# A graph layer's edge loop: two edges of one target in one partition, and gathers without a wait for TensorE

## The chip, the cores and the metric

The kernel runs on one core of one Trainium2 chip. The metric is device microseconds of one execution. Engines are named as the profile names them: PE (TensorE's matmuls) and PEld (its weight loads), DVE (VectorE), ACT (ScalarE), POOL (GpSimd, which issues the indirect gathers) and SP (SyncE, which issues the other DMAs).

## The reference

12500 nodes have rows x of 128 floats. The 412500 edges are 200000 drawn pairs in both directions and one self loop for each node, sorted by their target dst. What is computed, cut to what matters:

```python
theta = x[dst] - x[src]
w = sigmoid(relu(theta @ W1 + b1) @ W2 + b2)
agg = segment_sum(w * theta, dst)
indeg = segment_sum(ones, dst)
out = layernorm(x + agg + indeg * (x @ W4 + b4))
```

A self loop has theta = 0, so it adds nothing to agg and one to indeg.

## The kernel before

**Tables.** theta @ W1 is the difference of two table rows. A first stage of 13 chunks makes two tables in DRAM: z, with x W1 beside x for each node (1 KB a row), which is gathered by source, and y3d, with x W1 cut into three bfloat16 parts, which is read by target.

**Steps and blocks.** The edges are cut into parts; one part is one step s of the main loop (NS = 352 steps). The first PLAIN = 20 parts hold 1024 edges each (FIRST and MORE), every later part CE = 1182. Two steps are a block b, whose targets fit a window of WB = 96 nodes. Steps s < NH = 8 gather from x itself, later ones from z.

**Placing.** For the later parts `place` (a generator whose pieces are strewn over the loop, three sets of up to 128 steps) thins each part of 1182 edges down to 1024 places, eight tiles (K = 8) of 128 partitions. It drops the self loops and takes out 128 "hot" edges, 64 from each of two ranges of 1152 sources, whose rows come from tables in SBUF by products with one-hot matrices (`hot_fetch`, L891) instead of a gather. What is left is squeezed together by eight passes of shifts (L565 to L581), and the sources (src_i), places in the window (rel) and places among the part's targets (rows_d in DRAM) are written out.

**A step.** For step s the engines do this:

- POOL: `gather` issues eight indirect DMAs (L340), 128 rows of z each, into one of NZ = 9 row buffers (zbuf), for step s + AHEAD = 4 in the order of the code.
- ACT: `one_hot` makes oh for step s + 2 in two passes (L772, L773) over the broadcast places (to_all, one DMA a block): 123 partitions by 9 x 128, eight tiles and one for the hot edges. There are two buffers oh.
- PE: `spread_y` multiplies oh with y3, a product for each of the eight tiles (L781): each edge's target row of x W1, in ph (PSUM, two buffers).
- DVE: `one_hot_w` makes ow (L791), 128 x 8 x 96, the edge's place in the block's window, in two buffers. `weights` subtracts the gathered rows from ph (L824), applies relu and W2 (L825) and sums (L828). ACT makes the gate from the sums by a sigmoid (L829, L830). `weigh` multiplies the gathered x with the gate into wx (L839, two buffers of 8 x 130 columns: 128 values, the gate and a constant 1).
- PE: `add_up` adds ow times wx into pa (L940), a product for each tile with 130 columns, and one for the hot edges (`hot_rows` L904 and L905, `hot_weights` L915 to L920). At a block's odd step a last product carries the former block's sums over (a times sh). `total` copies pa to a (ACT, L951), and `normalize` (L963 to L990) finishes the rows of the block two before and stores them.

**Order.** The code gives instructions a priority by their place; a scheduler fixes each engine's order at build time, except for SP's, which is written out by hand. Every engine then works its own queue in order, and a waiting instruction holds what stands behind it. Two rules are set by hand for gathers: they keep their own order, and from step NH + LAG on the gather of tile k of step s waits for a step of TensorE's work that was entered for (s - LAG, k), with LAG = 6. `step` enters these: the block's own transpose (L707), the last of spread_y's products, hot_rows' product (L905) and add_up's last. At the end a flag computed by the kernel from its own assumptions (`bad`) chooses whether a general path, `any_dst`, runs instead; line L1111.

Of the kernel before, what the change touches and what calls it, by code (L numbers as in the profile page):

```python
# [19 lines left out]
P = 128  # L20
D = 128
K = 8
BE = K * P
# [7 lines left out]
NZ = 9  # L31
AHEAD = 4
LB = 6
LAG = 6
# [8 lines left out]
RW = BE + HK  # L43
# [5 lines left out]
CE = 1182  # L49
# [7 lines left out]
def gnn_resnorm(  # L57
# [45 lines left out]
    KT = -(-TAIL // P)  # L103
    assert NS == NF + 1 and NS % SUB == 0 and TAIL <= BE and SUB == 2 and N < BIG

# [36 lines left out]
    def load(i):  # L142

        s0, n, full = sets[i]
        es = ep.tile([P, CE], I32, name="es")
        ed = ep.tile([P, CE + 1], I32, name="ed")
        e0 = E1 + (s0 - PLAIN) * CE
        if full < n:
            nc.vector.memset(es[:n, :], 0)
            nc.vector.memset(ed[:n, :], N)  # L150
# [68 lines left out]
    oh_buf = [const.tile([P, K + 1, P], BF16, name=f"oh{i}") for i in range(2)]  # L219
# [78 lines left out]
    wx_buf = [const.tile([P, K, AW], F32, name=f"wx{i}") for i in range(2)]  # L298
# [19 lines left out]
    def tiles(s):  # L318
        return K if s < NF else KT

# [8 lines left out]
    steps_of = {}  # L329
    table_steps = []  # L330

    def step(s, i, ins):

        steps_of[s // SUB * SUB + i // K, i % K] = ins

    def gather(s):

        (src_i, _, _), i = set_of(s)
        for k in range(tiles(s)):
# [7 lines left out]
            if s - LAG >= NH and (s - LAG, k) in steps_of:  # L347
                waits.append((steps_of[s - LAG, k], mybir.DependencyClass.Sync))
# [92 lines left out]
    def place(i, ps, es, ed, bb):  # L441
# [9 lines left out]
        c = ep.tile([P, 6], F32, name="col")[:n]  # L451
# [9 lines left out]
        v.tensor_scalar(b[:full, 1:2], c[:full, 3:4], -1.0, float(CE - BE - HR * HS),  # L461
                        op0=OP.mult, op1=OP.add)
# [5 lines left out]
        t = ep.tile([P, CE], F32, name="et")[:n]  # L468
        nc.scalar.activation(t, ed[:, :CE], AF.Identity, scale=float(BIG), bias=c[:, 0:1])
        C = CE // 3  # L470
        for j in range(3):
            at = slice(j * C, (j + 1) * C)
            step = ps.tile([P, G, P], F32, name=bank).rearrange("p g d -> p (g d)")[:n, :C]
            v.tensor_sub(step, ed[:, j * C + 1:(j + 1) * C + 1], ed[:, at])
            q = ep.tile([P, P * G], F32, name="eq")[:n, :C]
            v.tensor_sub(q, es[:, at], ed[:, at])
            v.tensor_mul(q, q, step)
            v.scalar_tensor_tensor(t[:, at], step, 0.0, t[:, at], op0=OP.is_equal, op1=OP.mult)
# [11 lines left out]
        key = ep.tile([P, CE + 1], F32, name="ed")[:n, :CE]  # L490
# [3 lines left out]
        for r in range(HR):  # L494
            apart = aparts[r][:n]
            whole = CE // PM * PM
# [3 lines left out]
                apart.rearrange("p (o m) -> p o m", o=1).to_broadcast([n, CE // PM, PM]), op=OP.add)  # L500
            if whole < CE:
                v.tensor_tensor(key[:, whole:], t[:, whole:], apart[:, :CE - whole], op=OP.add)
# [32 lines left out]
        nc.sync.dma_start(rows_d[:n, BE:], hd[:, 1, :])  # L535
        hots[s0] = hot_s, hrel, n

        w = ep.tile([P, CE], I32, name="ew")[:n]
        C = CE // 6
        for j in range(6):  # L540
            at = slice(j * C, (j + 1) * C)
            pw = ps.tile([P, G, P], F32, name=bank).rearrange("p g d -> p (g d)")[:n]
            count = pw[:, :C]
            q = ep.tile([P, P * G], F32, name="eq")[:n]
            keep, out_ = q[:, :C], q[:, C:2 * C]
            v.tensor_scalar(keep, t[:, at], float(NOT * BIG), None, op0=OP.is_ge)
            v.scalar_tensor_tensor(w[:, at], t[:, at], float((2 * NOT - 1) * BIG), keep,
                                   op0=OP.min, op1=OP.mult)
            v.tensor_scalar(out_, keep, -1.0, 1.0, op0=OP.mult, op1=OP.add)
            v.tensor_tensor_scan(count, out_, most[:n].to_broadcast([n, C]),  # L550
                                 c[:, 4:5] if j else 0.0, op0=OP.add, op1=OP.min)
            v.tensor_copy(c[:, 4:5], count[:, C - 1:])
            move = out_.bitcast(I32)
            far_on = pw[:, C:2 * C]
# [6 lines left out]
        v.tensor_sub(b[:full, 10:11], c[:full, 4:5], c[:full, 3:4])  # L561
        v.tensor_scalar(b[:full, 10:11], b[:full, 10:11], -float(HR * HS), None, op0=OP.add)
        v.tensor_scalar(b[:full, 11:12], b[:full, 10:11], -1.0, None, op0=OP.mult)
        assert SW + HR * HS < LAST + P
        for r, m in enumerate([1 << r for r in range(7)] + [LAST]):  # L565
            u = ep.tile([P, CE], I32, name="ew" if r % 2 else "et")[:n]
            C = bits.shape[1] - m
            for c0 in range(0, CE, C):
                c2 = min(c0 + C + m, CE)
# [9 lines left out]
                if c2 == CE:  # L579
                    break  # L580
            w = u  # L581
        to = ep.tile([P, CE + 1], I32, name="ed")[:n, :BE]
        v.tensor_scalar(to, w[:, :BE], BIG.bit_length() - 1, 2 * NOT - 1,
                        op0=OP.logical_shift_right, op1=OP.bitwise_and)
        off = ep.tile([P, P * G], F32, name="eq").bitcast(BF16)
        nc.scalar.activation(off[:n], to, AF.Identity, bias=c[:, 1:2])
        nc.sync.dma_start(rows_d[:n, :BE], off[:n])
        yield
        t = ep.tile([P, CE], F32, name="et")[:n]
        nc.scalar.activation(t[:, :BE], to, AF.Identity, bias=c[:, 2:3])  # L590
        src_i = pp.tile([P, K, P], I32, name="src_i")
        rel = pp.tile([P, K, P], BF16, name="rel")
        f = ep.tile([P, CE], F32, name="es")[:n]
# [3 lines left out]
        for e, to in ((f, src_i), (t, rel)):  # L597
            for k0 in range(0, K, G):
                pt = ps.tile([P, G, P], F32, name=bank)
                for j in range(G):  # L600
                    nc.tensor.transpose(pt[:, j, :n], e[:, (k0 + j) * P:(k0 + j + 1) * P],
                                        ident[:n, :n])
                nc.scalar.activation(to[:, k0:k0 + G, :n], pt[:, :, :n], AF.Copy)
                yield
        placed[s0] = src_i, rel, rows_d

    with tc.manual_schedule(engines={SP}), tc.tile_pool(name="work", bufs=2) as wp, tc.tile_pool(
# [94 lines left out]
        def own_u(b):  # L702
# [3 lines left out]
            step(b * SUB - 2, 2,  # L706
                 nc.tensor.transpose(pw[:, :WB], d["xw"][:WB], ident[:WB, :WB]))  # L707
# [42 lines left out]
        def one_hot(s, half):  # L750


            n0, n1 = half * G, min(half * G + G, tiles(s))
# [21 lines left out]
        def spread_y(s):  # L775

            d = parts[s]
            b, h = divmod(s, SUB)
            d["ph"] = ps_h.tile([P, K, D], F32, name="ph")
            for k in range(tiles(s) if s >= NH else 0):  # L780
                got = nc.tensor.matmul(d["ph"][:, k, :], d["oh"][:, k, :], blocks[b]["y3"][h],  # L781
                                       start=True, stop=True)
                if k == tiles(s) - 1:
                    step(s - 1, 9 * (1 - h), got)

        def one_hot_w(s):

            n = tiles(s)
            (_, rel, _), i = set_of(s)
            ow = wp.tile([P, K, WB], F32, name="ow", bufs=2)[:, :n, :]  # L790
            nc.vector.tensor_tensor(ow, iota_f.to_broadcast([P, n, WB]),  # L791
                                    rel[:, :n, i:i + 1].to_broadcast([P, n, WB]), op=OP.is_equal)
            parts[s]["ow"] = ow
# [17 lines left out]
        def weights(s):  # L811
            n = tiles(s)
            d = parts[s]
            zs = rows_of(s)
            xs = zs if s < NH else zs[:, :, D:]
            wx = wx_buf[s % 2]
            h = d["ph"]
            if s < NH:
                both(s)
                nc.vector.scalar_tensor_tensor(  # L820
                    h, d["ph"], 0.0, w2_f.to_broadcast([P, K, D]), op0=OP.max, op1=OP.mult)
            else:
                ph = d["ph"][:, :n, :]
                nc.vector.tensor_sub(ph, ph, zs[:, :n, :D])  # L824
                nc.vector.scalar_tensor_tensor(  # L825
                    h[:, :n, :], ph, 0.0, w2_f.to_broadcast([P, n, D]), op0=OP.max, op1=OP.mult)
            lg = wp.tile([P, K], F32, name="lg")
            summed = nc.vector.tensor_reduce(lg[:, :n], h[:, :n, :], AX.X, OP.add)  # L828
            nc.scalar.activation(gate[:, s % 2, :n], lg[:, :n], AF.Sigmoid, bias=b2_c)  # L829
            nc.scalar.activation(wx[:, :n, D], lg[:, :n], AF.Sigmoid, bias=b2_c)  # L830
            return summed

        def weigh(s):

            n = tiles(s)
            zs = rows_of(s)
            xs = zs if s < NH else zs[:, :, D:]
            w = gate[:, s % 2, :n].rearrange("p (k e) -> p k e", e=1)
            return nc.vector.tensor_tensor(wx_buf[s % 2][:, :n, :D], xs[:, :n, :],  # L839
                                           w.to_broadcast([P, n, D]), op=OP.mult)  # L840
# [57 lines left out]
        def hot_rows(s):  # L898
# [6 lines left out]
            got = nc.tensor.matmul(px[:, 0, :], d["oh"][:, K, :], blocks[b]["y3"][h],  # L905
                                   start=False, stop=True)
            step(s - 2, K * h + 7, got)
# [14 lines left out]
        def add_up(s):  # L922

            n = tiles(s)
# [6 lines left out]
            terms = [(d["ow"][:, k, :], wx_buf[s % 2][:, k, :]) for k in range(n)]  # L931
# [7 lines left out]
            for i, (one, w) in enumerate(terms):  # L939
                summed = nc.tensor.matmul(pa, one, w, start=h == 0 and i == 0,  # L940
                                          stop=h == 1 and i == len(terms) - 1)
            step(s + 1, (13, 5)[h], summed)
# [3 lines left out]
        def total(b):  # L946
# [4 lines left out]
            nc.scalar.activation(a[:WB], pa, AF.Copy)  # L951
# [4 lines left out]
            d.update(a=a, sw=sw[:WB, 0:1], deg=sw[:WB, 1:] if b * SUB >= PLAIN else a[:WB, D + 1:])  # L956
# [92 lines left out]
        for s in range(NS + 1):  # L1049
# [33 lines left out]
            if s + 2 < NS and tiles(s + 2) > G:  # L1083
# [14 lines left out]
        with after(weighted):  # L1098
# [201 lines left out]
```

## Time and profile before

| | us |
|---|---|
| three runs: lowest, median, highest | 4624.53, 4624.89, 4639.22 |
| profiled execution, whole | 4628.1 |
| its span, first to last instruction | 4626.2 |
| busy: DVE | 3121.2 (67%) |
| busy: POOL | 2681.1 (58%) |
| busy: PE, PEld | 2636.8 (57%), 1988.8 (43%) |
| busy: ACT | 1603.8 (35%) |
| mean granted TensorE clock | 0.729 |

PE and PEld overlap. A share is a mean over the whole span; the set-up before the regular loop lasts some 470 us. An idle time in the groups is the time that the engine stood still just before such an instruction, and the name behind it is who ended most of it; "remote" is an update of a semaphore that the profile cannot put to an instruction, "issue" a wait that it does not show.

### The profile page before, as it was taken

What the parts mean: (1) busy time and instruction counts of PE and PEld (TensorE: products, weight loads), DVE (VectorE), ACT (ScalarE), POOL (GpSimd) and SP (SyncE); (2) the same over time, 40 slices, a digit from 0 to 9 for tenths busy, and PEclk for the clock granted to TensorE, in tenths of its full rate; (3) what the DMA queues carried; (4) which work ended last, traced back from release to release, by engine and by line L of the source; (5) the groups of instructions that cost most, each with busy time, mean ns of one, the idle gap of its engine ahead of it and who ended that gap; (6) DMA issues with size and microseconds to landing.
All of it is one profiled execution on the core that took longest, in us unless ns stands there. A gap on an engine that the chain in (4) does not pass through costs nothing. (4 is left out here: it accounts for less than half of the span.)

```text
span 4626.2 us, 47225 instructions
## 1 busy us (share of the span) xinstructions
PE 2636.8 (57%) x14207; PEld 1988.8 (43%) x14207; DVE 3121.2 (67%) x5030; ACT 1603.8 (35%) x3344; POOL 2681.1 (58%) x2824
## 2 busy tenths in 40 slices
PE   4355556665655555655565655556555556555555
PEld 4344344444444444444444444444444444444444
DVE  5676667777776666666777776777666566566666
ACT  4233333333333333333333333333333333333333
POOL 4415656666565566665556656656656565655663
PEclk6676777767777777777777777776777777777777
DMA  6303433443443344434333433434433443333432
GB/s 247 111 28 108 126 115 114 122 121 112 118 122 110 109 125 122 120 114 122 112 118 116 121 109 115 123 111 123 121 112 112 121 120 117 116 116 114 120 113 67
DMA packets 269164, 539.42 MB, mean 117 GB/s; under 512 B 101349, under 2 KB 152737, under 8 KB 267365
## 3 DMA queue, kind: packets, MB, share of 16 engines
q0 software_dynamic: 134096, 364.95, 27.2%
q1 hardware_dynamic: 132834, 164.97, 11.2%
q10 hardware_dynamic: 1970, 6.40, 0.5%
q8 instruction: 115, 1.88, 0.2%
q14 instruction: 149, 1.21, 0.1%
HBM read 504.19 MB, written 31.90 MB: 116 GB/s over the span
## 5 line engine op out<-in xcount | busy, mean ns | idle before, releaser
L340 POOL DMA_INDIRECT zbuf<-z,src_i x2655 | 2524.2, 951 | 1645.1 <-issue 695.5
L940 PE MATMUL pa<-wx,ow 128*96 128x130 f32 x5630 | 1125.8, 374 | 847.3 <-ACT a L951 339.9
L940 PEld LDWEIGHTS pa<-wx,ow 128*96 128x96 f32 x5630 | 1006.2, 238 | 953.9 <-ACT a L951 366.8
L839 DVE TENSOR_TENSOR wx<-zbuf,fix 128x1024 f32<-128x1024 f32 x352 | 427.3, 1214 | 601.0 <-ACT fix L829 449.2
L772 ACT ACTIVATE oh<-to_all,away 123x1152 bf16<-123x1152 bf16 x332 | 415.7, 1252 | 689.8 <-remote 350.2
L891 PE MATMUL pd<-of,tabs 128*128 128x512 bf16 (+1 forms) x2322 | 543.1, 385 | 91.2 <-issue 90.7
L791 DVE TENSOR_TENSOR ow<-fix,rel 128x768 f32<-128x768 f32 x352 | 333.5, 947 | 300.3 <-remote 296.7
L884 DVE TENSOR_TENSOR of<-hot_src,fix 128x1536 bf16<-128x1536 f16 (+1 forms) x258 | 422.2, 1690 | 10.8 <-remote 8.6
L828 DVE TENSOR_REDUCE lg<-ph 128x8 f32<-128x1024 f32 x352 | 427.0, 1213 | 0.0
L824 DVE TENSOR_TENSOR ph<-ph,zbuf 128x1024 f32<-128x1024 f32 x344 | 420.2, 1222 | 8.8 <-issue 3.2
L904 PE MATMUL pw<-wni,xT 128*128 128x256 f32 x664 | 301.7, 548 | 210.1 <-ACT wxh L918 106.2
L825 DVE SCALAR_TENSOR_TENSOR ph<-ph,w_r 128x1024 f32<-128x1024 f32 x344 | 420.7, 1223 | 0.0
L891 PEld LDWEIGHTS <-tabs 128*128 128x128 bf16 x2322 | 233.1, 101 | 363.3 <-issue 150.5
L773 ACT ACTIVATE oh<-oh 123x1152 bf16<-123x1152 bf16 x332 | 384.1, 1157 | 6.4
L781 PE MATMUL ph<-y,oh 128*128 128x128 bf16 x2751 | 261.0, 244 | 180.5 <-DVE lg L828 121.3
L781 PEld LDWEIGHTS <-oh 128*128 128x128 bf16 x2751 | 215.7, 111 | 246.5 <-issue 211.5
L915 DVE SCALAR_TENSOR_TENSOR hh<-pw,w_r 128x128 f32<-128x128 f32 x332 | 92.6, 279 | 285.5 <-PE pw L905 181.2
L940 PE MATMUL pa<-a,sh 96*96 96x130 f32 x350 | 106.2, 398 | 287.7 <-issue 85.4
L963 ACT ACTIVATE pw<-xw,sw 96x128 f32<-96x128 f32 x176 | 64.6, 367 | 545.2 <-issue 241.4
L904 PEld LDWEIGHTS pw<-wni,xT 128*128 128x128 f32 x664 | 142.7, 266 | 246.4 <-ACT wxh L918 135.9
L895 ACT ACTIVATE xT<-pd 128x512 f32<-128x512 f32 (+1 forms) x86 | 50.1, 582 | 481.6 <-PE pd L891 388.4
L951 ACT ACTIVATE a<-pa 96x130 f32<-96x130 f32 x176 | 47.8, 272 | 459.4 <-remote 398.5
(257 smaller groups left out, 2925.5 us busy)
## 6 DMA issues: line engine op xcount, KB each, us to landing
to_all<-off_d SPq DMA_DIRECT2D x166, 576.0 KB
zbuf<-z,src_i POOLq DMA_INDIRECT x2655
z<-zbuf SPq DMA_DIRECT2D x12, 1024.0 KB
y<-y3d SPq DMA_DIRECT2D x342, 30.8 KB
y3d<-tabs SPq DMA_DIRECT2D x12, 768.0 KB
xw<-in_x_dram SPq DMA_DIRECT2D x176, 48.0 KB
out_dram<-o SPq DMA_DIRECT2D x176, 48.0 KB
zbuf<-in_x_dram ACTq DMA_DIRECT2D x12, 512.0 KB
```

Source lines behind the costliest of these rows:

```text
L340: ins = nc.gpsimd.indirect_dma_start(out=rows_of(s)[:, k, :], out_offset=None, in_=z if s >= NH else x, in_offset=IndirectOffsetOnAxis(ap= ...
L772: nc.scalar.activation(gap, at[:3 * SW, h], AF.Abs, bias=away[:3 * SW])
L773: nc.scalar.activation(gap, gap, AF.Relu, scale=-1.0, bias=1.0)
L781: got = nc.tensor.matmul(d["ph"][:, k, :], d["oh"][:, k, :], blocks[b]["y3"][h], start=True, stop=True)
L824: nc.vector.tensor_sub(ph, ph, zs[:, :n, :D])
L825: nc.vector.scalar_tensor_tensor(h[:, :n, :], ph, 0.0, w2_f.to_broadcast([P, n, D]), op0=OP.max, op1=OP.mult)
L828: summed = nc.vector.tensor_reduce(lg[:, :n], h[:, :n, :], AX.X, OP.add)
L839: return nc.vector.tensor_tensor(wx_buf[s % 2][:, :n, :D], xs[:, :n, :], w.to_broadcast([P, n, D]), op=OP.mult)
L884: nc.vector.tensor_tensor(of, hot_src[:, r, lo:hi].rearrange("p (o e) -> p o e", o=1).to_broadcast([P, T, hi - lo]), nid[:, g * T:(g + 1) ...
L891: nc.tensor.matmul(px, tabs[:, r, g * T + t, c, :], of[:, t, :], start=g == 0 and t == 0 and c == 0, stop=g == 2 and t == T - 1 and c == 2)
L904: nc.tensor.matmul(px[:, :2, :], xT, wni, start=True, stop=False)
L940: summed = nc.tensor.matmul(pa, one, w, start=h == 0 and i == 0, stop=h == 1 and i == len(terms) - 1)
```

## The change

**Pairs.** In a later part two edges of one target share a partition: a partition holds J = 4 pairs instead of K = 8 single edges, still eight gathered rows. To make every target's number of edges even, `place` keeps the self loop of a target whose remaining number is odd, and a mark says so; a spare place is added to the part (WE = CE + 1). The kept loop's column in wx that counts edges is set by a mark of 0 or 1 (a new copy on ScalarE, four values a partition). As loops are kept, a part takes fewer edges: CE = 1156, and there are 360 steps.

**What follows in a step.** oh has five tiles instead of nine (640 columns), to_all is shorter in proportion, spread_y has four products, and DVE's subtraction reads each of the four twice. ow has 4 x 96 columns, in four buffers. add_up has four products of 2 x 130 columns, so pa has two halves; `total` copies one half, and a new `finish`, placed in the next odd step between weights and weigh, adds the other half on VectorE and makes 1 + w. wx has three buffers (NW).

**Gathers.** `step`, LAG and the waits of gathers for TensorE's steps are gone; gathers still keep their own order and wait for their row buffer.

The core of the diff:

```diff
-    oh_buf = [const.tile([P, K + 1, P], BF16, name=f"oh{i}") for i in range(2)]
+    oh_buf = [const.tile([P, K, P], BF16, name=f"oh{i}") for i in range(2)]
...
-    wx_buf = [const.tile([P, K, AW], F32, name=f"wx{i}") for i in range(2)]
+    wx_buf = [const.tile([P, K, AW], F32, name=f"wx{i}") for i in range(NW)]
...
-            if s - LAG >= NH and (s - LAG, k) in steps_of:
-                waits.append((steps_of[s - LAG, k], mybir.DependencyClass.Sync))
...
-        C = CE // 6
-        for j in range(6):
+        C = -(-WE // 8)
+        for j in range(8):
...
             v.tensor_scalar(keep, t[:, at], float(NOT * BIG), None, op0=OP.is_ge)
+            v.scalar_tensor_tensor(mark, t[:, at], float(BIG), keep, op0=OP.is_ge, op1=OP.add)
+            v.tensor_scalar(mark, mark, -1.0, 1.0, op0=OP.mult, op1=OP.add)
...
+            v.tensor_tensor_scan(odd[:, 1:], mark, keep, c[:, 5:6] if j else 0.0,
+                                 op0=OP.mult, op1=OP.add)
+            v.tensor_copy(c[:, 5:6], odd[:, m:])
+            v.scalar_tensor_tensor(mark, mark, 0.0, odd[:, :m], op0=OP.is_equal, op1=OP.mult,
+                                   accum_out=c[:, 6 + j:7 + j])
+            v.tensor_add(keep, keep, mark)
...
-                gap = oh[:3 * SW]
+                gap = oh[:3 * SW, :J + 1]
...
-            for k in range(tiles(s) if s >= NH else 0):
-                got = nc.tensor.matmul(d["ph"][:, k, :], d["oh"][:, k, :], blocks[b]["y3"][h],
-                                       start=True, stop=True)
...
+            n, k0 = (K, 0) if s < PLAIN else (pairs(s), J)
+            for k in range(n if s >= NH else 0):
+                nc.tensor.matmul(d["ph"][:, k0 + k, :], d["oh"][:, k, :], blocks[b]["y3"][h],
+                                 start=True, stop=True)
...
-            ow = wp.tile([P, K, WB], F32, name="ow", bufs=2)[:, :n, :]
+            for k0 in range(0, K if s < PLAIN else J, J):
+                ow = wp.tile([P, J, WB], F32, name="ow", bufs=4)
...
+                    y = y[:, J:J + n, :].rearrange("p (o k) d -> p o k d", o=1)
+                    y = y.to_broadcast([P, 2, n, D])
...
+                nc.vector.tensor_sub(to, y, zy)
...
+            if s >= PLAIN:
+                (_, rel, _), i = set_of(s)
+                nc.scalar.activation(wx[:, J:, D + 1:], rel[:, J:, i:i + 1], AF.Copy)
...
-                bd["pa"] = ps_l.tile([P, AW], F32, name="pa")
+                bd["pa"] = ps_l.tile([P, 2, AW], F32, name="pa")
...
+                wx = wx.rearrange("p (h k) d -> p k h d", h=2)
+                terms = [(d["ow"][0][:, k, :], wx[:, k]) for k in range(pairs(s))]
...
+                nc.scalar.activation(a[:WB], pa[:, 1, :], AF.Copy)
...
+        def finish(b):
...
+            if b * SUB >= PLAIN:
+                nc.vector.tensor_add(a[:WB], a[:WB], d["pa"][:WB, 0, :])
             carry[0] = a
...
+            if s % SUB and b:
+                finish(b - 1)
```

More of the change, by code (lines that the diff above doesn't have):

```diff
@@ L48 @@
 HOT = P * HT
-CE = 1182
+CE = 1156
+WE = CE + 1
 PM = 31
@@ L148, in load @@
         if full < n:
-            nc.vector.memset(es[:n, :], 0)
+            for r in range(HR):
+                nc.vector.memset(es[:n, r::HR], r * HOT)
             nc.vector.memset(ed[:n, :], N)
@@ L939, in add_up @@
             for i, (one, w) in enumerate(terms):
-                summed = nc.tensor.matmul(pa, one, w, start=h == 0 and i == 0,
-                                          stop=h == 1 and i == len(terms) - 1)
-            step(s + 1, (13, 5)[h], summed)
+                to = pa if len(w.shape) == 3 else pa[:, 0, :]
+                nc.tensor.matmul(to, one, w, start=h == 0 and i == 0,
+                                 stop=h == 1 and i == len(terms) - 1)
             if h:
```

204 lines of the change are left out of this document (115 added, 89 removed).

## The prediction

> **What bounds the kernel now.** I read the page's totals first, to see whether an engine is full.
>
> ```profile
> PE 2636.8 (57%) x14207; PEld 1988.8 (43%) x14207; DVE 3121.2 (67%) x5030; ACT 1603.8 (35%) x3344; POOL 2681.1 (58%) x2824
> ...
> PEclk6676777767777777777777777776777777777777
> ```
>
> None is: the loop waits. Its pace is the spacing of VectorE's product L839, once a step: its 21st start lies at 471.5 us, its 352nd at 4606.9, so 331 spacings of 12.49 us, 4135 us in all. (Between 3000 and 3500 us POOL issued 321 gathers, 40 steps of eight: 12.5 us a step again.) Second, the groups by shape:
>
> ```profile
> L772 ACT ACTIVATE oh<-to_all,away 123x1152 bf16<-123x1152 bf16 x332 | 415.7, 1252 | 689.8 <-remote 350.2 <-PE pw L905 193.9 <-issue 62.1
> ...
> L773 ACT ACTIVATE oh<-oh 123x1152 bf16<-123x1152 bf16 x332 | 384.1, 1157 | 6.4
> ...
> L766 ACT ACTIVATE oh<-pd,away 123x512 bf16<-123x512 bf16 x40 | 27.3, 683 | 44.5 <-remote 18.5 <-PE ph L807 15.3 <-issue 6.1
> ...
> L767 ACT ACTIVATE oh<-oh 123x512 bf16<-123x512 bf16 x40 | 25.1, 628 | 1.0
> ```
>
> The second number after the bar is ns of one; these rows price the one-hot at two widths. Third, the list of waits (who waited for what: us in total, times, longest):
>
> ```profile
> DVE wx L839 <- ACT fix L829: 449.2, 107, 10.4
> POOL zbuf L340 <- PE pd L707: 422.6, 72, 16.1
> ACT a L951 <- remote: 398.5, 56, 16.1
> ...
> DVE ow L791 <- remote: 296.7, 55, 16.1
> ```
>
> POOL waits for TensorE, so the gathers are ahead of the work; VectorE's L824, the first to read gathered rows, sat idle for a landing for under 1 us in all. "Remote" hides the real brake. The timeline of one block shows it:
>
> ```profile
> 976.43 0.75 PE L940 MATMUL pa<-a,sh 96*96 96x130 f32 x2 [1.23 <-issue]
> ...
> 977.24 0.95 POOL L340 DMA_INDIRECT zbuf<-z,src_i  x1 [0.30 <-issue]
> 978.49 0.95 POOL L340 DMA_INDIRECT zbuf<-z,src_i  x1 [0.30 <-issue]
> 979.74 0.95 POOL L340 DMA_INDIRECT zbuf<-z,src_i  x1 [0.30 <-issue]
> ...
> 983.68 0.96 DVE L791 TENSOR_TENSOR ow<-fix,rel 128x768 f32<-128x768 f32 x1 [6.87 <-remote]
> 983.83 0.28 ACT L951 ACTIVATE a<-pa 96x130 f32<-96x130 f32 x1 [6.92 <-remote]
> ...
> 984.07 0.94 POOL L340 DMA_INDIRECT zbuf<-z,src_i  x1 [3.38 <-remote]
> ...
> 984.56 1.22 DVE L824 TENSOR_TENSOR ph<-ph,zbuf 128x1024 f32<-128x1024 f32 x1
> ```
>
> The block's carry product ends at 977.18 by its row. L791 and L951, which need only that, start 6.5 us later, and so does POOL's next gather. In between no engine but POOL works. TensorE's completions arrive late while gathers run. By the semaphore events (some are lost, so these are bounds) 292 of 342 completions came within 40 ns of the row's end while POOL stood still, and 380 of 1053 while it generated a gather.
>
> **The base.** The profiled execution took 4628.1 us (span 4626.2), 0.07% over the median 4624.89. 4628.1 - 4135.4 leaves 492.7 us outside the 331 spacings.
>
> **More steps.** A part holds 1156 edges, not 1182, so there are 360 steps and 339 spacings: at today's 12.49 us, +99.9 us. Break-even with everything below is 12.15 us a step. POOL's gathers grow from 2815 to 359 x 8 + 2 = 2874; at 0.951 + 0.305 us that is 10.05 us a step, under the pace.
>
> **ScalarE.** From 123x512 to 123x1152 the first pass grows by 569 ns, the second by 529; 123x640 is then 797 and 734, 0.88 us less than 2.41. The new copy of four 0/1 marks costs about 0.22 (L955's 96x2 took 197 ns, L829's 128x8 259). Net -0.66 us a step, of work that stands ahead of the gate L829 in ScalarE's queue. VectorE waits for L829 in 107 steps of 352, mostly because ScalarE itself stood at a late completion: I count half, -0.33; bounds 0 and -0.66.
>
> **VectorE.** 128x1024 takes 1222 ns and 128x768 947, 1.07 ns an element: the half one-hot is 0.54, -0.41 us. The new sum of the two halves of a block costs what L964 does on 96x128, 0.287 us a block, +0.14 a step. Net -0.27, on the path, since VectorE is the fullest engine. The subtraction L824 reads four products twice at the same 1024 elements: nothing. A repeated operand there has no row; L791 repeats two and takes 1.23 ns an element against L824's 1.19, so plus or minus 0.04 us.
>
> **The wait that moves.** All 56 long waits of L791 are in odd steps, for the buffer that the block's carry product frees. Four half buffers free L791. But in the built order the new sum stands in VectorE's queue of odd steps right behind L824, and needs ScalarE's L951, which needs the same completion. So VectorE still stops; L825, the reduce, the gate and L839 stand behind it, and ScalarE's next copy (the 1 + w) waits for the sum too. What is gained is L791 and L824 done before the stop, 0.95 + 1.22; what is lost is L951 and the hop, about 0.44 (983.68 against 984.11). -1.73 us in 56 of 166 blocks is -97 us, -0.29 a step; bounds: nothing, and -1.73 in every block, -0.87.
>
> **TensorE.** Four one-hot products fewer (244 ns each by the rows, 56 to 107 ns apart in bursts). The weighted sum has half as many products of twice the columns: 16 of L940's matmuls stream as many columns as 8 of 260. By mean rows 16 x 374 = 5.98 us against 8 x 548 (L904's 256 columns) = 4.38: -1.6 us of busy time, 0 by columns. I take 0: the waits above end with a completion that comes us after the work.
>
> **Gathers without TensorE's steps.** POOL now stops only for a row buffer, which VectorE's L839 of nine steps before frees, all eight gathers at once; today a gather waits for TensorE's steps of six steps before, spread over the step. I price this at nothing, because nobody waits for gathered rows; if that cover is gone the price is the second rival. The broadcast to_all shrinks from 576 to 320 KB a block, and SP issues the same transfers a block: nothing.
>
> **Set-up.** The placing of a set has eight pieces of some 14 operations instead of six of eight; about 2.9 us a piece today, 4.2 then: (8 x 4.2 - 6 x 2.9) = 16 us of VectorE a set. For the second and third VectorE's idle third hides it; the first lies ahead of the loop: +16.
>
> **Sum.** 12.49 - 0.27 - 0.29 - 0.33 = 11.60; 339 x 11.60 + 492.7 + 16 = 4441 us. With the bounds: 10.69 gives 4133, and 12.22 (VectorE's work alone) 4651.
>
> **Two rules weighed.** The Trainium skill (Perfetto Trace Analysis, Per-engine timelines) says that TensorE's row ends are estimated and that the event goes out when PSUM has acknowledged. By that rule the empty 6.5 us may be TensorE's own work; the trace bears it out only in that completions come on time when POOL rests, so I give it a chance of its own below. The Trainium skill (TensorE: Matmul & The Clock Gate, The HAM clock gate) says that an idle window of about 3.4 us halves the clock; the trace agrees, the granted clock was 0.50 from 977.2 to 983.6.
>
> **Rivals.**
> 1. The late completions set the pace and what is shed lies in their shadow: 12.49 stays, 339 x 12.49 + 508.7 = 4743, slower. For: the three engines stand still together. Against: they stand behind two buffers that grow from two to three (wx) and to four (ow). 0.17.
> 2. Bursts, slower: L839 frees eight gathers at once, POOL runs 10.05 us without a pause, TensorE's completions pile up behind it, and each step ends with a drained stop of 3.38 us, the one in the timeline: 13.43, 5061 us. For: 64% of completions were not on time under a gather. Against: today stops come in nearly every step too (1887.8 us idle before gathers less 2815 x 0.305 = 1029, 2.9 a step). It decides when VectorE's next L839 takes more than 10.05 us. 0.16.
> 3. Hidden TensorE work that halves with the products: half of L951's 398.5 us is 199, 0.59 a step: 11.01, 4241. 0.08.
> 4. POOL becomes the bound, when completions no longer hold anyone: 10.05, 3916. Against: 9 buffers at most. 0.06.
> 5. TensorE's shorter work leaves it at half clock always: 18 of L940's matmuls took 3.76 us at 0.50 and 2.21 at 1.00; with the clock at 0.73 over the loop about half run at full clock now, 0.5 x 1.55 = 0.78 us at most, two thirds on the path 0.5: 12.1, 4611. 0.04.
> 6. The kernel's own test fails and the general path runs, thousands of us. Counting edges in the inputs, no part keeps more than 1020 of the 1024 places: 0.01.
>
> **How the numbers follow.** The forecast has 0.48. Faster: 0.44 of it with rivals 3 and 4, 0.58. Slower: rivals 1, 2, 6, and the rest above 4642, 0.38. Within 0.3% (14 us, about what a measurement of this kernel can tell from no change): 0.04. The range runs from below the forecast's bound to above rival 1, 4100 to 4830; outside lie rivals 2, 4 and 6 in part. The likeliest case alone is 4133 to 4651.
>
> **What would show it.** ScalarE's one-hot at about 797 and 734 ns, VectorE's at 540, L839 spaced 11.6 us. The waits should show the new sum waiting for ScalarE in odd steps where L791 waited. POOL's stops should be ended by VectorE. It is wrong if the spacing is 12.2 or more, by rival 1 if the idle stretches keep their number, by rival 2 if they grow to 8 us and more.

## The result and the profile after

The changed kernel takes 5021.41 us (median of 4 runs, 4987.72 to 5022.97) against 4624.71 us for the kernel before: a ratio of 1.084, with a 95% interval of 1.078 to 1.089. It is slower, where 4441 us and faster were forecast. The profiled execution took 5022.97 us.

The totals on the page of the changed kernel (busy time, share of the span, instructions) answer to the first fence of the prediction:

```profile
PE 2550.9 (51%) x10431; PEld 1593.6 (32%) x10431; DVE 3118.1 (62%) x5542; ACT 1434.3 (29%) x3757; POOL 2747.0 (55%) x2883
...
PEclk6566767766666676776776676667777777777777
```

TensorE has 3776 products fewer and ScalarE 170 us of work less, and VectorE's busy time is the same to 3 us. So the work did shrink, and the idle time grew more: every engine's share fell. The spacing of VectorE's product of rows and gates (L876 now, L839 before) is 13.22 us where 12.49 was; 339 x 13.22 = 4483 us, and 540 us lie outside.

The groups of the changed kernel (busy us, mean ns of one, idle us just before them and what ended most of it):

```profile
L349 POOL DMA_INDIRECT zbuf<-z,src_i x2714 | 2588.9, 954 | 1957.9 <-issue 770.5 <-DVE sh L975 370.8 <-DVE wx L876 331.8
...
L856 DVE TENSOR_TENSOR ph<-ph,zbuf 128x1024 f32<-128x1024 f32 x352 | 428.8, 1218 | 6.0 <-issue 3.0 <-PE ph L807 2.4 <-PE pd L788 0.2
...
L797 ACT ACTIVATE oh<-to_all,away 123x640 bf16<-123x640 bf16 x340 | 280.3, 824 | 556.3 <-remote 173.7 <-PE pw L942 168.3 <-issue 103.8
...
L817 DVE TENSOR_TENSOR ow<-fix,rel 128x384 f32<-128x384 f32 x380 | 205.5, 544 | 26.0 <-remote 23.8 <-PE pd L732 1.7 <-PE pw L628 0.5
...
L868 ACT ACTIVATE wx<-rel 128x4 f32<-128x4 bf16 x340 | 71.1, 209 | 917.1 <-remote 576.4 <-PE pa L980 180.4 <-issue 118.6
...
L1001 DVE TENSOR_TENSOR a<-a,pa 96x130 f32<-96x130 f32 x170 | 47.0, 277 | 310.1 <-ACT a L993 226.6 <-issue 65.7 <-ACT wxh L952 17.4
```

The durations came out as estimated: the one-hot's first pass 824 ns (estimate 797), the half one-hot on VectorE 544 (540), the mark copy 209 (220), the new sum 277 (287). The subtraction that first reads gathered rows (L856) still waits 6 us in the whole run, so no row arrives late. But two rows carry idle time that the prediction did not have: the mark copy L868, 917 us ahead of an operation of 0.2 us, and the sum L1001, 310 us. POOL's stops are now ended by VectorE, as forecast.

The list of waits of the changed kernel (us in total, times, longest):

```profile
DVE wx L876 <- ACT fix L863: 905.3, 168, 23.1
ACT wx L868 <- remote: 576.4, 97, 18.9
...
POOL zbuf L349 <- DVE sh L975: 370.8, 65, 10.2
...
ACT a L993 <- remote: 301.2, 28, 16.6
```

VectorE's wait for the gate doubled, from 449 to 905 us. The timeline of one block shows how (start, duration, and in brackets the idle time before):

```profile
2199.75 0.75 PE L980 MATMUL pa<-a,sh 96*96 96x130 f32 x2 [5.92 <-DVE wx L876]
...
2199.86 0.95 POOL L349 DMA_INDIRECT zbuf<-z,src_i  x1 [0.30 <-issue]
...
2200.52 1.22 DVE L856 TENSOR_TENSOR ph<-ph,zbuf 128x1024 f32<-128x1024 f32 x1
...
2211.14 0.95 POOL L349 DMA_INDIRECT zbuf<-z,src_i  x1 [0.30 <-issue]
2216.03 0.28 ACT L993 ACTIVATE a<-pa 96x130 f32<-96x130 f32 x1 [15.79 <-remote]
...
2216.33 0.29 DVE L1001 TENSOR_TENSOR a<-a,pa 96x130 f32<-96x130 f32 x1 [14.59 <-ACT a L993]
```

It is the picture of the prediction's timeline, drawn out. The carry product ends at 2200.5; ScalarE, which needs only that, starts at 2216.0. POOL generates one gather every 1.25 us throughout, the last at 2211.14, and the completion arrives 3.9 us after that one's row ends. In the prediction's block 6.5 us were lost, here 15.5.

Two counts from the trace are used below. **Late stretches**: the time from the end of TensorE's last row to a completion that comes over 0.8 us later, each row once, summed. Before: 902 us in 209 stretches, 4.3 us each on average; after: 1308 in 226, 5.8 us each. That is 406 us more, about what the time grew by (395 us between the profiled executions). The count is rough: two profiles of one kernel on chips of one kind, e2 and e15, give 1137 and 1241, so a difference of some 100 us between two runs is not read as one. **POOL's stops** (gaps over 0.6 us between gathers, from 470 us on): before 249 stops of 3.6 us with 10.5 gathers between two, after 176 stops of 6.6 us with 15.2, every one at the first gather of a step.

### The profile page after: what moved, and what is told of

It is laid out like the page before. It is cut to its first block, busy times and chain, and to the rows that moved or that the text cites. A ratio compares the mean times of both kernels' runs of the same rounds, so it can differ in the third digit from the quotient of the medians.

```text
span 5021.2 us, 39957 instructions
## 1 busy us (share of the span) xinstructions
PE 2550.9 (51%) x10431; PEld 1593.6 (32%) x10431; DVE 3118.1 (62%) x5542; ACT 1434.3 (29%) x3757; POOL 2747.0 (55%) x2883
## 4 chain that ended last, share of the span: by engine, by line
PE 27%; another core or an unknown queue 26%; issue 16%; DVE 16%; ACT 11%; DMA 1%; POOL 1%; SPq 1%; DVEq 0%; ACTq 0%; POOLq 0%
PE pa L980 13%; PE pd L928 4%; PE pw L941 3%; DVE wx L876 3%; DVE ph L857 2%; ACT oh L797 2%; PE pd L736 2%; ACT oh L798 2%; DVE lg L862 2%; DVE ph L856 2%; DVE of L921 1%; PE ph L807 1%; PE pd L732 1%; ACT wxh L953 1%
## 5 line engine op out<-in xcount | busy, mean ns | idle before, releaser
L349 POOL DMA_INDIRECT zbuf<-z,src_i x2714 | 2588.9, 954 | 1957.9 <-issue 770.5
L980 PE MATMUL pa<-wx,ow 128*96 128x260 f32 (+1 forms) x3034 | 1033.1, 502 | 332.0 <-DVE wx L876 168.1
L876 DVE TENSOR_TENSOR wx<-zbuf,fix 128x1024 f32<-128x1024 f32 x360 | 438.0, 1217 | 1110.9 <-ACT fix L863 905.3
L980 PEld LDWEIGHTS pa<-wx,ow 128*96 128x96 f32 x3034 | 630.3, 226 | 626.4 <-issue 215.7
L857 DVE SCALAR_TENSOR_TENSOR ph<-ph,w_r 128x1024 f32<-128x1024 f32 x360 | 439.3, 1220 | 37.0 <-remote 32.3
L797 ACT ACTIVATE oh<-to_all,away 123x640 bf16<-123x640 bf16 x340 | 280.3, 824 | 556.3 <-remote 173.7
L856 DVE TENSOR_TENSOR ph<-ph,zbuf 128x1024 f32<-128x1024 f32 x352 | 428.8, 1218 | 6.0 <-issue 3.0
L868 ACT ACTIVATE wx<-rel 128x4 f32<-128x4 bf16 x340 | 71.1, 209 | 917.1 <-remote 576.4
L732 PE MATMUL pd<-ident,xw 96*128 96x96 f32 x175 | 65.6, 375 | 421.7 <-ACT xT L932 319.5
L807 PE MATMUL ph<-y,oh 128*128 128x128 bf16 x1453 | 166.9, 240 | 182.9 <-DVE lg L862 89.5
L798 ACT ACTIVATE oh<-oh 123x640 bf16<-123x640 bf16 x340 | 250.0, 735 | 9.0
L1001 DVE TENSOR_TENSOR a<-a,pa 96x130 f32<-96x130 f32 x170 | 47.0, 277 | 310.1 <-ACT a L993 226.6
L980 PEld LDWEIGHTS pa<-a,sh 96*96 96x96 f32 x358 | 64.4, 232 | 544.6 <-DVE sh L975 391.0
L817 DVE TENSOR_TENSOR ow<-fix,rel 128x384 f32<-128x384 f32 x380 | 205.5, 544 | 26.0 <-remote 23.8
```

What stands on the lines that cost most here:

```text
L349: ins = nc.gpsimd.indirect_dma_start(out=rows_of(s)[:, k, :], out_offset=None, in_=z if s >= NH else x, in_offset=IndirectOffsetOnAxis(ap= ...
L797: nc.scalar.activation(gap, at[:3 * SW, h], AF.Abs, bias=away[:3 * SW])
L798: nc.scalar.activation(gap, gap, AF.Relu, scale=-1.0, bias=1.0)
L807: nc.tensor.matmul(d["ph"][:, k0 + k, :], d["oh"][:, k, :], blocks[b]["y3"][h], start=True, stop=True)
L856: nc.vector.tensor_sub(to, y, zy)
L857: nc.vector.scalar_tensor_tensor(ph, ph, 0.0, w2.to_broadcast(list(ph.shape)), op0=OP.max, op1=OP.mult)
```

## The experiments

Three theories. A: the gathers' waits for TensorE's steps (called the pace here) were what kept TensorE's completions coming, and losing them is the cost. B: the mark copy, which the built order puts in ScalarE's queue ahead of the gate of the step before, waits there for TensorE and holds that gate up. C: VectorE's stop at the new sum. All ratios are to the kernel before on the same chip, because that kernel itself took 4743 to 4747 us on the chips of e1 to e8 and e13 to e16, and 4626 to 4629 us on those of e9 to e12, e17 and e18. The changed kernel itself was run only on chips of the second kind (1.084, and 1.083 as e17), so beside e1 to e8 it can be set by its ratio alone, not by its us or its spacing.

**e1: the kernel before without the pace.**

```diff
-            if s - LAG >= NH and (s - LAG, k) in steps_of:
-                waits.append((steps_of[s - LAG, k], mybir.DependencyClass.Sync))
```

> The kernel before, with one thing taken out: its gathers no longer wait for TensorE's steps; edges, one-hots and products are as before. Theory A (the pace: without it POOL sends each freed buffer's eight gathers in one go, and TensorE's completions come late in longer stretches): slower, spacing of L839's products 13.2 to 13.4 us instead of 12.49, 331 x 13.2 + 493 = 4860 to 4930 us. Theory B (the mark copy L868, which stands in ScalarE's queue ahead of an older gate and waits there for TensorE): this kernel has no such copy, so 4625 us within 1%. Theory C (the new sum L1001 on VectorE): not here either, 4625 us within 1%.

Measured: 5386.88 us, ratio 1.136 (1.133 to 1.139); repeated as e16, 1.137 (1.134 to 1.139). Spacing 14.66 us, late stretches 1561 us, 181 stops of 8.9 us. No other part of the change is in it, so the pace alone is worth 643 us to the kernel before. That is the sign of A and more than its size; B and C fall for this kernel. Its list of waits has POOL's stops ended by VectorE, one longest of 18.8 us, as in the changed kernel:

```profile
POOL zbuf L340 <- DVE owh L918: 1209.4, 130, 18.8
```

**e2: the changed kernel with the pace put back** (the same waits, LAG 6, on the same places).

> The changed kernel with the gathers waiting again for TensorE's steps of six steps before, at the same places as in the kernel before. Theory A: the spacing falls from 13.22 us to about that of the prediction's sum without rivals, 11.6 to 12.2 us, 339 x 11.6 + 540 = 4470 to 4680 us, and POOL's stops are ended by TensorE. Theory B: ScalarE's idle time ahead of L868 stays near 900 us and the time near 5000 us. Theory C: VectorE's idle time ahead of L1001 stays and the time stays near 5000 us.

Measured: 4832.57 us, 1.019 (1.016 to 1.022); again as e15, 1.016 (1.014 to 1.018). Spacing 12.67, 246 stops of 4.1 us. POOL's stops are again ended by TensorE. By the ratios most of the loss is gone, so B and C, which left the time near 5000 us, are not the main cause; but the spacing misses A's 11.6 to 12.2. Theory B's row stays (groups of e2):

```profile
L879 ACT ACTIVATE wx<-rel 128x4 f32<-128x4 bf16 x340 | 70.9, 208 | 1019.9 <-remote 632.1 <-issue 174.8 <-PE pa L993 133.1
```

**e3: the mark copy behind its own step's gate, no pace; e4: the same with the pace.**

```diff
-            nc.scalar.activation(filled(wx[:, :, D:D + 1], s), lgs, AF.Sigmoid, bias=b2_c)
+            g = nc.scalar.activation(filled(wx[:, :, D:D + 1], s), lgs, AF.Sigmoid, bias=b2_c)
...
+                with after([g]):
+                    nc.scalar.activation(wx[:, J:, D + 1:], rel[:, J:, i:i + 1], AF.Copy)
```

> The changed kernel, in which the copy of the marks (L868) stands in ScalarE's queue behind the gate of its own step instead of ahead of the gate of the step before. Theory B: the 917 us idle ahead of it go, VectorE's wait for the gate falls from 905 to about the 449 us of before, 1.35 us a step: 13.22 - 1.35 = 11.9, 339 x 11.9 + 540 = 4570 us. Theory A: ScalarE's idle time turns up ahead of its next instruction that waits for TensorE, and the time stays within 1% of 5021 us. Theory C: the same as A.

> Both: the changed kernel with the gathers' waits for TensorE's steps and with the mark copy behind its gate. Theory A: as the run with the waits alone, within 1%. Theory B: as the run with the copy moved alone, within 1%. If both hold a part, this one is the fastest of the four, near the prediction's 11.6 us a step, about 4470 us.

Measured: e3 5151.14 us, 1.088 (1.083 to 1.092); e4 4723.27 us, 0.996 (0.994 to 0.997). In both the copy's idle time is 0.0 us and VectorE's wait for the gate is down to 437 us. With the pace that is worth 109 us against e2 (4832.57 - 4723.27). So both theories hold a part, but e4's spacing is 12.40 us, not near 11.6. Without the pace no gain shows: the ratio is 1.088 where the changed kernel has 1.084 on chips of the other kind. In e3 the stop turned up at the sum, by way of ScalarE, as A said.

```profile
L1002 DVE TENSOR_TENSOR a<-a,pa 96x130 f32<-96x130 f32 x170 | 47.3, 278 | 752.6 <-ACT a L994 655.1 <-issue 90.0 <-ACT wxh L953 7.0
```

This is the row of the sum in e3's groups: 753 us idle, where the changed kernel had 310; ScalarE's copy that it needs waited 797 us, where it was 301. The difference between e3 and e4, 428 us, is the pace.

**e5: seven row buffers in turn instead of nine, no pace.** `rows_of` takes its buffer modulo 7.

> The changed kernel without the gathers' waits, mark copy behind its gate (as e3, 1.0876 of the time before), but with seven row buffers in turn instead of nine, so that POOL can be about six steps ahead as with the waits and not eight. Theory A1 (the lead is what hurts: gathers that run further ahead rob later work of its pauses): the time falls to that with the waits, 0.99 to 1.01 of before. Theory A2 (the burst hurts: eight gathers from one release and no pause among them, however far ahead): 1.07 to 1.11 of before, and POOL's stops stay at the first gather of a step.

Measured: 5151.53 us, 1.085 (1.082 to 1.088), as e3. POOL stops as seldom (168 stops of 7.8 us). All of them are at the first gather of a step. A shorter lead alone does not help: A1 falls. A2's range and its sign come true, but whether the burst itself is the cause is for e9.

**e6: e4 with the sum of the halves behind the weigh product.**

```diff
-            if s % SUB and b:
-                finish(b - 1)
...
             if s < NS - 1:
-                weigh(s)
+                w = weigh(s)
+            if s % SUB and b:
+                with after([w] if s < NS - 1 else []):
+                    finish(b - 1)
```

> As e4 (waits restored, mark copy behind its gate, 0.9956 of before), and the sum of a block's two halves is put in VectorE's queue behind the weigh product of the odd step, not ahead of its first use of gathered rows. Theory C (VectorE's stop at the sum is on the path, the prediction's step of the wait that moves): the 374.8 us that it waited for ScalarE's copy go, up to 1.1 us a step, 0.92 to 0.96 of before. Shadow theory (TensorE's completions come late anyway, and the next reader of them waits instead): 0.985 to 1.005, and the 375 us turn up at other instructions that wait for TensorE or for ScalarE.

Measured: 4673.59 us, 0.986 (0.983 to 0.989); again as e14, 0.984 (0.982 to 0.987). The sum's idle time fell from 428 us in e4 to 1.6, the time by 50. That is the edge of the shadow theory's range and far from theory C's: most of the stop lay beside completions that were late anyway. The lists of waits show where it reappears, at other readers of TensorE, VectorE's L964 above all, which waited 86.8 us in e4. First e4, then e6:

```profile
ACT xT L944 <- remote: 661.5, 66, 26.7
```

```profile
ACT xT L944 <- remote: 777.0, 54, 30.2
DVE hh L964 <- PE pw L954: 578.8, 74, 31.9
```

**e7 and e8: three quarters of the gathers left out**, in the kernel before without the pace, and in e3.

```diff
+            if s >= NH + NZ and k % 4:
+                continue
```

> The kernel before without the gathers' waits (as e1, 1.1356 of before), and from the tenth loop step with gathers on it issues two of eight gathers a step and leaves the other six out; all other instructions stay. If TensorE's completions come late because POOL generates gathers: the stretches in which a completion comes over 0.8 us late sum to under 400 us instead of 1561, and the time falls below 0.90 of before. If they have another source: over 1000 us of them, and at least 1.05 of before.

> The changed kernel without the gathers' waits, mark copy behind its gate (as e3), with the same six of eight gathers left out. Against e7 it shows what the merging is worth where completions are on time. If the prediction's terms for VectorE and ScalarE hold (-0.27 and -0.33 us a step, the wait that moves gone with the late completions): the spacing is 0.6 us below that of e7, and with eight more steps and the longer set-up the time is about 110 us below. If these terms were never on the path: the same spacing within 0.1 us, and about 100 us above e7.

Measured: 3486.97 us (0.735) and 3359.26 us (0.708). Their totals, e7 and then e8:

```profile
PE 2462.2 (71%) x14127; PEld 1875.9 (54%) x14207; DVE 3096.5 (89%) x5030; ACT 1610.9 (46%) x3344; POOL 769.9 (22%) x815
...
PEclk6667787887778888888887788888788888888887
```

```profile
PE 2343.8 (70%) x10349; PEld 1502.0 (45%) x10431; DVE 3088.6 (92%) x5542; ACT 1405.6 (42%) x3757; POOL 786.9 (23%) x831
```

Late stretches are down from 1561 to 55 us in e7 and from 1372 to 53 in e8, and the loop has not one of them: those left lie in the set-up and at the end. TensorE does the same work as in e1 and e3, so the stretches are made by the gathers. VectorE, with the same work, is 89 and 92% busy: now an engine bounds the kernel. Here the change's own worth shows: the spacings are 9.12 us in e7 and 8.49 in e8, 0.63 less, near the 0.60 of the prediction's two terms, and e8 is 128 us faster in spite of its eight steps more. Where it comes from is another matter (lists of waits, e7 and then e8):

```profile
DVE hh L915 <- PE pw L905: 114.4, 80, 3.7
...
DVE wx L839 <- ACT fix L829: 93.7, 72, 3.2
```

```profile
DVE wx L879 <- ACT fix L865: 79.8, 79, 24.8
```

VectorE's wait for the gate hardly fell, from 93.7 to 79.8 us. What fell is its wait for a product of TensorE with the hot rows, 114.4 us in e7 and 12.3 in e8.

**e9: three gathers of a step wait for VectorE's steps** of six steps before (L856, L857 and the reduce of the changed kernel), in place of TensorE's.

> As e3 (changed kernel, mark copy behind its gate, 1.0876 of before), but three of the eight gathers of a step wait for instructions of VectorE six steps before (the subtraction, the relu product, the reduce), where e4's waits for TensorE gave 0.9956. Theory S (spread: what counts is that the eight gathers are not sent in one go): about 1.00, POOL's stops then ended by VectorE in the middle of a step. Theory T (tie to TensorE: only a POOL that stands still exactly because a completion of TensorE is late lets that completion through): 1.06 to 1.10, and the stretches of late completions still sum to over 1300 us.

Measured: 4952.2 us, 1.068 (1.066 to 1.071), against 1.083 for the changed kernel on a chip of the same kind (e17). POOL now stops nearly as often as with the pace (227 stops, 11.8 gathers between two), yet the late stretches sum to 1416 us. Its groups name VectorE behind the stops:

```profile
L351 POOL DMA_INDIRECT zbuf<-z,src_i x2714 | 2578.5, 950 | 1926.0 <-issue 725.9 <-DVE ph L861 284.4 <-DVE ph L860 263.0
```

The stops stand at the third, sixth and eighth gather of a step, where they mostly stand in e4 too, so the bursts are broken up as there. Spreading the gathers is not enough; what they wait for matters. Theory S falls, theory T's range holds.

**e10 and e11: e6 with a lag of five and of seven steps** (`LAG = 5`, `LAG = 7`).

> As e6 (waits restored, mark copy and sum moved back, 0.9859 of before), the gathers waiting for TensorE's steps of five steps before instead of six. If a closer tie makes the late stretches shorter: 0.95 to 0.98. If gathers then come too late: VectorE's subtraction shows waits for DMA queues of more than 100 us, and the time is 1.00 or more.

> As e6, the gathers waiting for TensorE's steps of seven steps before. If a closer tie is better, this is the worse side: 1.00 to 1.04, toward the 1.0876 without the waits. If six was only a cautious value: within 1% of e6.

Measured: 4640.24 us, 1.003 (1.002 to 1.004), and 4628.64 us, 1.000 (0.999 to 1.001), the latter again as e18 with 1.000 (0.998 to 1.002). Their spacings, 12.15 and 12.13, lie close to e6's 12.24, and so do the late stretches (856 and 893 against 914). Between five and seven steps the lag hardly matters, and a closer tie does not shorten the stretches. Nor do the gathers come too late with five: the subtraction waits 13.6 us for the DMA queue, not over 100. These ratios can't be set beside e6's, since the chips are of the two kinds.

**e12: half the bytes.** As e3, but from the tenth loop step with gathers on each row brings 128 floats of x in place of 256 of the table.

> As e3 (without the gathers' waits), with as many gathers of 128 rows each, but from the tenth loop step with gathers on each row brings 128 floats of x instead of 256 of the table, half the bytes; the other half of the buffer keeps old rows. If POOL's making of the descriptors holds TensorE's completions back: late stretches still sum to over 1100 us, 1.03 to 1.09 of before. If it is the rows' own traffic: about half of e3's 1372 us, and 0.90 to 0.96 of before.

Measured: 5090.35 us, 1.099 (1.096 to 1.102), late stretches 1492 us: on the descriptors' side, and beyond its range. The groups of e12 have the gather at the same price as with all the bytes:

```profile
L349 POOL DMA_INDIRECT zbuf<-in_x_dram,src_i x2714 | 2572.4, 948 | 2048.7 <-issue 742.8 <-DVE ph L857 708.1 <-DVE a L1003 306.7
```

The gathers' queue moved 193 MB where it moved 373 in e3, and its packets took 13.4% of the DMA engines' time where they took 25.0%. So it is the making of the descriptors, or the number of rows, not the bytes that the rows bring. The Trainium skill (Perfetto Trace Analysis, DMA Instruction — SWDGE (GPSIMD)) says that such a row ends when the last descriptor is written, not when the data has moved; 948 ns for half the bytes beside 954 for all agrees.

**e13: more gathers tied to TensorE**, beside e14 (e6 again), e15 (e2 again) and e16 (e1 again).

```diff
+                if i in (0, 2, len(terms) - 1):
+                    step(s + 1, (13, 5)[h] - (2, 1, 0)[min(i, 4) // 2], summed)
```

(and the first product of the hot rows and of the one-hot's, in the same way).

> As e6, with more of the gathers waiting for TensorE: besides the last product of a group also the first and third of the weighted sum, the first of the hot rows and the first of the one-hot's, each at the matching gather of six steps later (three to five of eight gathers instead of two or three). Tie theory (POOL standing still on TensorE lets late completions through): the late stretches sum to under 800 us against 914 in e6, 0.96 to 0.985 of e14's time. If the waits of e6 already do all that waits can: within 1% of e14.

> e6 again, beside the others. If the gain was one of the chips (before took 4743 us there, 4625 on others): 0.998 to 1.005 on a chip where before takes 4625 us. If it is one of six steps against five and seven: 0.98 to 0.99 anywhere.

> e2 again: the changed kernel with the gathers' waits alone. 1.019 where before takes 4743 us. Where it takes 4625 us: 1.02 if the pace is what the prediction missed most, 1.05 and more if it explains less than half of the 8.4%.

> e1 again: the kernel before without the gathers' waits. 1.13 to 1.14 as in e1 if the chip does not matter; 1.16 and more if before is the only one of these kernels that the chip changes.

Measured: e13 4689.43 us, 0.988 (0.986 to 0.991), 19 us slower than e14. POOL stops much oftener (343 stops of 2.6 us, 7.9 gathers between two), and the late stretches hardly move, 887 against 903. More waits of the kind do no more than the ones of before, as the second reading had it: the tie theory's forecast falls. It also shows that shorter chains of gathers, 7.9 where e14 has 12, do not help by themselves. e14, e15 and e16 came to a chip of e1's kind again (before 4747 us), so what they were to tell of the other kind stays unanswered.

**e17 and e18: the changed kernel, and e11, once more.**

> The changed kernel as it is. Where before takes 4625 us: 1.084 again. Where before takes 4743 us: 1.08 if the chip slows both alike; 1.06 if only the kernel before is slower there.

> e11 again (waits for TensorE's steps of seven steps before, mark copy and sum moved back). Where before takes 4743 us: 0.98 to 0.99, as e6, if the chip makes the difference; 1.00 if seven steps do. Where before takes 4625 us: 1.000 as in e11.

Measured: 1.083 (1.079 to 1.086) and 1.000 (0.998 to 1.002), both where the kernel before takes 4629 us. So the changed kernel was not measured where before takes 4743 us, nor e1 to e6 where it takes 4625.

## Why the prediction was wrong

**The step that failed: "Gathers without TensorE's steps … I price this at nothing."** Its reason was true and stayed true: nobody waits for gathered rows (L856, 6.0 us). But the pace served something else. It made POOL wait for TensorE, and TensorE's completions are late where POOL makes eight gathers a step and on time where it makes two (e7, e8). The price is 643 us in the kernel before (e1) and 428 us between e4 and e3, 1.09 us a step, where the sum had 0. The warning was on the table: the prediction itself counted 64% late completions under a gather against 15% with POOL at rest, and then let the change take POOL's rests away at no cost.

**The second rival came near, by more than its size, but not by all of its mechanism.** It gave 13.43 us and 5061 us; measured were 13.22 and 5021. What it said of POOL came true: freed by VectorE, eight gathers go at once, POOL runs on (15.2 gathers between two stops where 10.5 were), and completions pile up. That the burst is what delays them was not borne out: e9 breaks the bursts up and keeps its late stretches. Its details were off too. There is not a drained stop of 3.38 us in each step but a stop of 6.6 us in about every second one; the kernel before had one in about three steps of four, not "in nearly every step"; and the stretches, which were to grow to 8 us and more, grew from 4.3 to 5.8 on average. So luck has a part in how near its time came, but it deserved far more than 0.16.

**ScalarE, -0.33: no wait was named for the mark copy.** Its duration was right, but what it waits for, at the place where it stands, was not looked at. It writes the row buffer of the weighted sum, which TensorE must have read, and it stands ahead of an older gate. With the pace in place this costs 0.27 us a step (12.67 to 12.40, e2 to e4); without it no gain shows, and the next reader of TensorE waits instead.

**The wait that moves, -0.29: nothing was gained.** The half buffers did free the one-hot (26 us idle, 300 before), but the sum took over with 310 us. Moving it behind the weigh product brought 50 us, 0.16 a step (e6).

**VectorE -0.27: right. ScalarE -0.33: right as work, but not by the path.** Where completions are on time, e8 against e7 gives -0.63 for the sum of -0.60. Over the regular loop VectorE's busy time fell from 8.38 to 8.12 us a step, 0.26. ScalarE's fell by 0.70, for a forecast of 0.66. But VectorE's wait for the gate, which was to fall by 0.33, fell from 0.25 to 0.22. Most of what is left of the 0.63 is the wait for the hot rows' product, from 0.35 to 0.04. That the sum fits so well is partly luck, and which part of the change brought TensorE's product sooner was not tested. The set-up was right too: 339 x 8.49 = 2878 of e8's 3362.0 us leaves 484, 331 x 9.12 = 3020 of e7's 3490.0 leaves 470, so +14 for +16. In the changed kernel 48 us are added outside the loop's spacings; e1, with the old set-up and on a chip of the other kind, already has 39 more there.

**Together:** 339 x (13.223 - 11.60) = 550 us, and 32 more outside than the sum had, make 4441 into 5023. The repairs e2, e4 and e6 take the spacing down to 12.67, 12.40 and 12.24, e11 to 12.13. The kernel before has 12.49 on e11's kind of chip, so with the repairs 0.36 of the forecast 0.89 us a step is seen, and the eight steps more use it up, as the break-even of 12.15 said. About 0.5 us a step is still not seen then. e6 shows late stretches of 914 us in it, so rival 1, what is shed lies in the shadow of late completions, fits this rest; that it is the whole of it was not tested.

**Other rivals.** Rival 5: the granted clock fell, 0.729 to 0.695, but it followed the idle time: with e7's short gaps it is 0.80, with the same products as in e1 (0.69). The first rule weighed in the prediction left open whether the empty stretch might be TensorE's own work (the Trainium skill, Perfetto Trace Analysis, Per-engine timelines: its row ends are estimated). The same work ends on time with fewer gathers, so the amount of it is not the reason; whether the gathers hold up the products or only the news of their end, no run tells apart. As for the second rule weighed, the trace agrees less than the prediction says: the granted clock was 1.00 until 975.2 us and 0.50 from there, so it fell 2 us before the empty stretch began.

**What stays open.** Why waits for TensorE's steps shorten the stretches and those for VectorE's do not (e9), while more of the former do no more (e13), was not settled; that a POOL stopped by the late completion itself lets it through is only argued. e7 and e8 take away gathers and shorten their chains at once, and which of the two clears the stretches was not separated, except that shorter chains with all the gathers did not (e13). Nor is it known why the kernel before takes 2.5% longer on some chips. With the pace and both repairs the change is worth 1.5% on one kind of chip (e6, e14); its twin with a lag of seven makes no difference on the other (e11, e18). No version was shown to beat the kernel before on both.

## What to carry to other kernels

A wait that seems to hold back an engine with time to spare may be there for someone else: before removing it, ask what that engine's activity does to the others, not only whether its product is needed sooner. When a trace shows completions late in the presence of one engine and on time without it, do not price a change of that engine's rhythm at nothing, and test it by leaving part of its work out. And of each new small operation look up its place in the queue: 0.2 us of work in front of an older gate cost 0.27 us a step here.

## What the runs showed of the hardware

With POOL generating indirect gathers of 128 rows one behind the other (0.95 us each, every 1.25 us), completions of TensorE reached waiting engines up to 15 us and more after the end of their rows as the profile has it. They did so at half the bytes a row too (1492 us of late stretches), and hardly at all with a quarter of the gathers, two a step (55 and 53 us, none of it in the loop). With all of the gathers VectorE was at most 67% busy in any of these kernels; with a quarter it reached 92%. And one and the same kernel took 4626 us on some chips and 4743 on others, 2.5% more, with every run of a chip within 0.6% of its median.
